# Moving the two halves of the weighted values in an attention pipeline on TensorE

## The chip, the cores and the metric

The kernel runs on one NeuronCore of a Trainium2 chip. The metric is the device time of one execution, in microseconds (us); lower is better.

## What is computed

The reference is a chain of four blocks on an input of 2 x 1024 tokens with 128 features: a two-layer transformer block with full attention, a two-layer block with local attention, a windowed attention with latent tokens, and a mixture of experts. The change is in the first block alone. Each of its layers computes, for each of the 2 sequences:

```python
xl = _ln(x, ln1_g, ln1_b)
q = (xl @ wq + bq).reshape(b_, s_, NH, DPH)          # NH = 2 heads of DPH = 64
k, v = ...                                           # likewise, from wk, bk and wv, bv
q, k = ...                                           # rotary factors, q / sqrt(DPH)
probs = jax.nn.softmax(jnp.einsum('bqhd,bkhd->bhqk', q, k), axis=-1)
att = jnp.einsum('bhqk,bkhd->bqhd', probs, v).reshape(b_, s_, h_)
x = x + att @ wo
xl2 = _ln(x, ln2_g, ln2_b)
hid = xl2 @ w1 + b1
hid = hid * jax.nn.sigmoid(1.702 * hid)
return x + hid @ w2
```

All of it is in float32.

## The kernel before

Block 1 (class `BlockA`) handles 2 layers x 2 sequences x 8 query tiles of 128 rows, 32 tiles in that order. For each tile, the following steps exist:

- `score` (L372) multiplies the tile's queries with all 1024 keys for both heads, into two PSUM tiles of 1024 columns, and VectorE takes the rows' negated maxima (L378).
- `exp(h)` (L384) is ScalarE's exponential of head h, with the row sums as a by-product.
- `turn(h, j)` (L395) transposes half j of head h's 1024 probabilities on TensorE, four 128 x 128 pieces into one PSUM bank. ScalarE copies the halves with j = 0 to SBUF (L398), VectorE those with j = 1 (L400).
- `value(j)` (L407) multiplies the transposed probabilities of key tiles 4j to 4j+3 with `v`: eight matmuls for both heads, each head in one half of the array's columns. Both halves add into one PSUM bank; `value(0)` starts the sum and `value(1)` ends it.
- `keep` (L415) copies the bank to `us` on ScalarE. With every fourth tile it starts the chain `after`.

Between these steps lies the other work on four tiles at a time, which also runs on TensorE. `after` is the rest of a layer: `project` (L442, product with `wo`; L447 and L450 on VectorE, L454 on GpSimd), a layer norm (statistics L289 and L290 on VectorE; L293 to L297 on GpSimd, where L297 writes the four normalised tiles `xn`), `turn` (L345 transposes, and ScalarE writes `hT`, L346), four times `up` (L467; L470 on ScalarE, L473 on GpSimd, L475 on VectorE), twice `down` (L488; L514 on VectorE). `prep` is the start of the next layer: the same norm, `features` (L345 and L346), `keys` (L314; L316, L317), `queries` (L321; L322) and `values` (L329; L334).

The order on each engine is the order in which the instructions are emitted, since the scheduler leaves TensorE, ScalarE, VectorE and GpSimd alone in this block. The class `Pipe` fixes it: each tile takes eight beats, and `later(beats, f, rank=...)` files a step for a later beat. In a beat the steps run by rank, the lowest first. The scores have rank 0, the chains' TensorE steps rank 5. Chain steps that need TensorE take a free beat among those that they are given, for instance `EARLY, LATE = (1, 2, 3, 5), (4, 5, 6, 7)`. So a step filed at beat 13 or 15 lies in beat 5 or 7 of the next tile's eight, and one filed at 16 lies in beat 0 of the tile after that.

PSUM has two places for scores (one for each head, used again by each tile) and four banks, called `bank`, which the transposes, the values and all steps of the chains share. A step that takes a bank waits until its former content has been read.

Of the kernel before, what the change touches and what calls it, by code (L numbers as in the profile page):

```python
# [108 lines left out]
class Pipe:  # L109
# [6 lines left out]
    def later(self, beats, f, bank=False, rank=0):  # L116
        at = self.now + beats
        if bank:
            among = range(1, 8) if bank is True else bank
            while at in self.taken or at % 8 not in among:  # L120
                at += 1
            self.taken.add(at)
        self.due.setdefault(at, []).append((rank, f))
# [54 lines left out]
class BlockA:  # L178
# [177 lines left out]
    def tile(self, l, b, qt):  # L356
        k, nc = self.k, self.k.nc
        q, kk, v = self.q[b], self.kk[b], self.v[b]
        later = self.pipe.later
        g = qt // 4  # L360
        st = self.st.setdefault((l, b, g), {})
        cut = slice(qt % 4 * P, qt % 4 * P + P)
        t = {}

        def score():
            assert ("ready", l, b, 1) in self.st or (l, b) == (0, 0)
            t["s"] = [k.ps_a.tile([P, S], F32, tag=f"s{h}", name=k.name("s")) for h in range(2)]
            for j in range(2):
                for h in range(2):
                    rows = slice(h * 64, (h + 1) * 64)  # L370
                    keys = slice(j * 512, (j + 1) * 512)
                    nc.tensor.matmul(  # L372
                        t["s"][h][:, keys], q[rows, qt * P : (qt + 1) * P], kk[rows, keys],
                        start=True, stop=True,
                    )
            t["nm"] = [self.small("nm", [1]) for _ in range(2)]
            for h in range(2):
                nc.vector.tensor_reduce(t["nm"][h], t["s"][h], AX.X, ALU.max, negate=True)  # L378

        def exp(h):  # L380
            if qt % 4 == 0 and h == 0:
                st["sums"] = self.p2.tile([P, 2, 4], F32, tag="sums", bufs=3, name=k.name("sums"))
            t["pr", h] = self.p2.tile([P, S], F32, tag="pr", bufs=4, name=k.name("pr"))
            nc.scalar.activation(  # L384
                t["pr", h], t["s"][h], AF.Exp, bias=t["nm"][h],
                accum_out=st["sums"][:, h, qt % 4 : qt % 4 + 1],
            )

        def turn(h, j):
            if h == j == 0:  # L390
                t["pT"] = self.p2.tile([P, 2, MT, P], F32, tag="pT", name=k.name("pT"))
            ps = self.bank()
            for i in range(4):
                at = (j * 4 + i) * P
                nc.tensor.transpose(ps[:, i * P : (i + 1) * P], t["pr", h][:, at : at + P], k.ident)  # L395
            dst = t["pT"][:, h, j * 4 : j * 4 + 4].rearrange("p i q -> p (i q)")
            if j == 0:
                nc.scalar.copy(dst, ps)  # L398
            else:
                nc.vector.tensor_copy(dst, ps)  # L400

        def value(j):
            if j == 0:
                t["u"] = self.bank()
            for kb in range(j * 4, j * 4 + 4):
                for h in range(2):
                    nc.tensor.matmul(  # L407
                        t["u"][h * 64 : h * 64 + 64, :P], v[:, kb, h * 64 : h * 64 + 64],
                        t["pT"][:, h, kb], start=(kb == 0), stop=(kb == MT - 1),
                    )  # L410

        def keep():
            if qt % 4 == 0:
                st["us"] = self.p2.tile([P, 512], F32, tag="us", name=k.name("us"))
            nc.scalar.copy(st["us"][:, cut], t["u"][:, :P])  # L415
            if qt % 4 == 3:
                self.after(l, b, g, st)

        for at, rank, f in (
            (0, 0, score), (3, 0, lambda: exp(0)), (4, 0, lambda: exp(1)), (9, 2, lambda: turn(0, 0)),  # L420
            (10, 2, lambda: turn(1, 0)), (11, 2, lambda: turn(0, 1)), (12, 2, lambda: turn(1, 1)),
            (13, 2, lambda: value(0)), (15, 2, lambda: value(1)), (16, -3, keep),
        ):
            later(at, f, rank=rank)

# [1820 lines left out]
```

## Time and profile before

| | |
|---|---|
| runs of the kernel, us | 1290.62, 1290.57, 1286.54 |
| median of the runs | 1290.57 us |
| the profiled execution: span from the first to the last instruction | 1288.7 us |
| mean granted TensorE clock in it | 0.962 |
| TensorE matmul busy | 1158.7 us (90%) |
| VectorE, ScalarE, GpSimd busy | 870.0, 646.3, 488.6 us (68%, 50%, 38%) |
| L407, weighted values | 73.1 us busy, 1024 matmul records |
| L395, transposes of the probabilities | 66.5 us busy, 512 records |
| L372, scores | 64.7 us busy, 256 records |

The profiled execution's own device time is not among the runs; its span of 1288.7 us is what the profile has of it, 1.9 us under the median of the runs. The profiler names the engines PE (TensorE, matmuls), PEld (its weight loads), DVE (VectorE), ACT (ScalarE), POOL (GpSimd) and SP (SyncE). A float32 matmul appears as two records, a float32 transpose as one. Matmuls are pipelined, and the ends of their records are modelled, so the time that a step costs TensorE is read from start to start. In the lines of a timeline, "x16" is a number of records that were merged, and brackets at the end name idle time of the engine and what ended it. PEclk is the clock that was granted to TensorE, 1.00 at full rate.

### The profile page before, as it was taken

The page shows a single profiled execution, that of the slowest core. Times are in us where ns is not written, and L with a number is a line of the kernel's source. Part 1 is how long each engine was busy: PE and PEld are TensorE (multiplying, and loading weights), DVE is VectorE, ACT ScalarE, POOL GpSimd, SP SyncE. Part 2 cuts the span into 40 slices and gives each one's busy share as a digit, 9 for nine tenths or more (in the row PEclk, how much of TensorE's full clock was granted, in tenths as well). Part 3 has the DMA queues.
Part 4 walks back from the last instruction along what each step waited for, and adds up shares of the span by engine and source line. Part 5 has one row for each costly group of instructions (what it writes and reads, how often), then busy time and mean ns, then how long its engine had stood idle before and what let it go on. Part 6 is the DMA issues. An engine that isn't in the chain of part 4 may idle for free.

```text
span 1288.7 us, 23486 instructions
## 1 busy us (share of the span) xinstructions
PE 1158.7 (90%) x9441; PEld 747.7 (58%) x9441; DVE 870.0 (68%) x1782; ACT 646.3 (50%) x1216; POOL 488.6 (38%) x565
## 2 busy tenths in 40 slices
PE   5999999999688999999999877989999978997798
PEld 3656766666356656666656634546555543433688
DVE  5556666555587776776777435556677979999763
ACT  5445455444355665665664545656665755441000
POOL 1523333232588776676686442221222211100000
PEclk9899999999899999999999988989998989999799
DMA  9000000000010000010100021000000000000000
GB/s 297 2 1 1 1 1 1 2 1 1 18 26 22 22 22 18 22 26 18 26 22 18 5 78 41 1 1 1 2 1 1 2 1 1 0 17 1 25 17 17
DMA packets 19840, 25.18 MB, mean 20 GB/s; under 512 B 2762, under 2 KB 13716, under 8 KB 19476
## 3 DMA queue, kind: packets, MB, share of 16 engines
q1 hardware_dynamic: 19076, 23.02, 6.4%
q8 instruction: 75, 1.23, 0.4%
q10 hardware_dynamic: 656, 0.66, 0.2%
q14 instruction: 33, 0.27, 0.1%
HBM read 13.32 MB, written 1.05 MB: 11 GB/s over the span
## 4 chain that ended last, share of the span: by engine, by line
PE 61%; DVE 23%; ACT 7%; POOL 5%; issue 4%; DMA 0%; DVEq 0%; POOLq 0%; ACTq 0%
PE big L1665 6%; PE mm L1748 5%; PE bank L407 4%; PE s L372 4%; PE bank L960 4%; PE s L727 3%; PE s L835 3%; PE bank L880 2%; PE s L1262 2%; PE s L1258 2%; PE bank L467 2%; PE tr L1299 2%; DVE nm L1267 2%; PE bank L488 2%; DVE nm L378 2%
## 5 line engine op out<-in xcount | busy, mean ns | idle before, releaser
L1267 DVE TENSOR_REDUCE nm<-s 128x4 f32<-128x1024 f32 (+1 forms) x64 | 71.0, 1152 | 60.1 <-PE s L1262 59.8
L378 DVE TENSOR_REDUCE nm<-s 128x1 f32<-128x1024 f32 x64 | 75.1, 1216 | 51.4 <-PE s L372 51.4
L1300 ACT COPY pT<-tr 128x512 f32<-128x512 f32 x120 | 70.0, 598 | 73.2 <-PE tr L1299 73.0
L774 POOL TENSOR_TENSOR t<-raw,tab 128x512 f32<-128x512 f32 x62 | 77.1, 1266 | 75.0 <-DVE raw L765 75.0
L1299 PE MATMUL tr<-ident,pr 128*128 128x128 f32 x480 | 77.2, 284 | 2.6 <-ACT pT L1300 2.3
L736 ACT ACTIVATE sq<-s 128x1024 f32<-128x1024 f32 x32 | 32.7, 1023 | 86.8 <-PE s L727 86.8
L384 ACT ACTIVATE pr<-s,nm 128x1024 f32<-128x1024 f32 x64 | 71.0, 1120 | 8.3 <-DVE nm L378 8.2
L395 PEld LDWEIGHTS bank<-ident,pr 128*128 128x128 f32 x512 | 57.4, 143 | 30.0 <-issue 22.5
L781 POOL TENSOR_TENSOR raw<-raw,tab 128x1024 f32<-128x1024 f32 x31 | 73.1, 2360 | 2.4
L788 POOL TENSOR_TENSOR raw<-raw,t 128x1024 f32<-128x1024 f32 x31 | 73.2, 2363 | 1.7
L407 PE MATMUL bank<-pT,v 128*64 128x128 f32 x1024 | 73.1, 287 | 0.7 <-DVE pT L400 0.2
L1674 ACT ACTIVATE hid<-big,cols 128x512 f32<-128x512 f32 x62 | 41.9, 687 | 60.4 <-PE big L1665 60.4
L1665 PE MATMUL big<-xTd,d_gate 128*128 128x512 f32 x128 | 67.1, 613 | 5.1 <-DVE r_above L1915 2.5
L1665 PE MATMUL big<-xTd,d_up 128*128 128x512 f32 x128 | 68.8, 628 | 2.7 <-DVE r_above L1912 2.0
L407 PEld LDWEIGHTS bank<-pT,v 128*64 128x64 f32 x1024 | 57.8, 142 | 22.6 <-issue 11.5
L398 ACT COPY pT<-bank 128x512 f32<-128x512 f32 x64 | 34.9, 587 | 68.3 <-PE bank L395 68.3
L1299 PEld LDWEIGHTS tr<-ident,pr 128*128 128x128 f32 x480 | 54.7, 144 | 21.0 <-issue 11.6
L395 PE MATMUL bank<-ident,pr 128*128 128x128 f32 x512 | 66.5, 280 | 0.0
L372 PE MATMUL s<-kk,q 64*128 64x512 f32 x256 | 64.7, 615 | 0.6 <-ACT pr L384 0.5
L1748 PEld LDWEIGHTS mm<-d_down,hid 128*128 128x128 f32 x496 | 61.0, 196 | 5.7 <-DVE xo L1779 1.9
L727 PE MATMUL s<-b_wqkv,hT 128*128 128x512 f32 x128 | 62.8, 613 | 1.7 <-ACT hT L694 1.3
L1748 PE MATMUL mm<-d_down,hid 128*128 128x128 f32 x496 | 61.7, 280 | 1.3 <-DVE xo L1779 1.3
(368 smaller groups left out, 2843.4 us busy)
## 6 DMA issues: line engine op xcount, KB each, us to landing
vs<-v SPq DMA_DIRECT2D x60, 130.0 KB, 2.2
b_wqkv<-in_L_ffn_wqkv_dram SPq DMA_DIRECT2D x2, 768.0 KB, 8.9
b_tab<-in_c_xpos_dram SPq DMA_DIRECT2D x1, 1024.0 KB, 8.0
d_up<-in_L_ffn_Wup_dram SPq DMA_DIRECT2D x1, 1024.0 KB, 5.4
d_gate<-in_L_ffn_Wgate_dram SPq DMA_DIRECT2D x1, 1024.0 KB, 7.3
out_dram<-xo SPq DMA_DIRECT2D x3, 256.0 KB, 2.3
rows<-in_rows_dram SPq DMA_DIRECT2D x1, 760.0 KB, 6.7
b_w<-in_L_ffn_w_dram SPq DMA_DIRECT2D x2, 341.0 KB, 7.7
```

Of the source, the lines that this page charges most:

```text
L372: nc.tensor.matmul(t["s"][h][:, keys], q[rows, qt * P : (qt + 1) * P], kk[rows, keys], start=True, stop=True,)
L378: nc.vector.tensor_reduce(t["nm"][h], t["s"][h], AX.X, ALU.max, negate=True)
L395: nc.tensor.transpose(ps[:, i * P : (i + 1) * P], t["pr", h][:, at : at + P], k.ident)
L407: nc.tensor.matmul(t["u"][h * 64 : h * 64 + 64, :P], v[:, kb, h * 64 : h * 64 + 64], t["pT"][:, h, kb], start=(kb == 0), stop=(kb == MT - 1),)
L727: nc.tensor.matmul(qk[:, cut], lhsT, k.b_wqkv[:, l, cut], start=True, stop=True)
L774: nc.gpsimd.tensor_tensor(t2[:, :, :, a : a + 32], r4[:, :, :, z : z + 32], tab(1)[:, :, None, a : a + 32].to_broadcast([P, 2, 8, 32]), AL ...
L781: nc.gpsimd.tensor_tensor(r4, r4, tab(0)[:, :, None, :].to_broadcast([P, 2, 8, 64]), ALU.mult)
L788: eng.tensor_tensor(flat, flat, t["t2"].rearrange("p j h d -> p (j h d)"), ALU.add)
L1267: nc.vector.tensor_reduce(nm[h], view[h], AX.X, ALU.max, negate=True)
L1299: nc.tensor.transpose(ps[:, c * P : (c + 1) * P], pr[:, c, t * P : (t + 1) * P], k.ident)
L1665: self.k.nc.tensor.matmul(ps, weights[:, rows], self.xT[:, cut], start=True, stop=True)
L1748: nc.tensor.matmul(sums[part][:, cols], hid[tp, h, c][:, e, cols], k.d_down[:, c + 8 * e, :], start=start and e == 0, stop=False,)
```

## The change

Both halves of the weighted values move to beat 16, with ranks just below that of the scores, and the copy `keep` moves from beat 16 to beat 17:

```diff
             (10, 2, lambda: turn(1, 0)), (11, 2, lambda: turn(0, 1)), (12, 2, lambda: turn(1, 1)),
-            (13, 2, lambda: value(0)), (15, 2, lambda: value(1)), (16, -3, keep),
+            (16, -1, lambda: value(0)), (16, -0.9, lambda: value(1)), (17, -3, keep),
         ):
             later(at, f, rank=rank)
```

Before, `value(0)` and `value(1)` of a tile stood in beats 5 and 7 after the next tile's scores, with the chains' steps between, behind and around them. After, both stand behind all chain steps of that stretch, in beat 0 of the tile after the next one, directly in front of its scores. No instruction is added or removed.

## The prediction

> **What bounds the kernel now.** I read the page first, then the engine's own timeline of TensorE over block 1 (22 to 322 us), then the timelines of DVE, ACT and POOL over one stretch of it, last the granted clock by one-microsecond stages. From the page:
>
> ```profile
> span 1288.7 us, 23486 instructions
> PE 5999999999688999999999877989999978997798
> L407 PE MATMUL bank<-pT,v 128*64 128x128 f32 x1024 | 73.1, 287 | 0.7 <-DVE pT L400 0.2
> ```
>
> Block 1 is the first ten slices (32.2 us each). TensorE is full there after the first slice, and the matmuls of the weighted values (L407) wait for almost nothing (0.7 us in all). So block 1 takes as long as TensorE's stream: a saving there counts in full, and so does a new hole. I call the stretch from one tile's scores (L372) to the next a round; there are 32 of them. The built order of both kernels shows rounds of four kinds that repeat: project (L442, then the turn L345 of a prep chain), queries (L314, L321, the chain's turn L345, L329, first up L467), up (three L467) and down (two L488). DVE, POOL and SP keep their order entirely, ACT too. Only TensorE's order and the PSUM banks' numbers change. Timeline of TensorE, a queries round and part of a down round (start, length to the modelled end, instruction, count; start to start is the price):
>
> ```profile
> 115.50 1.09 PE L407 MATMUL bank<-pT,v 128*64 128x128 f32 x16
> 116.52 0.68 PE L345 MATMUL bank<-ident,xn 128*128 128x128 f32 x4
> 117.04 1.06 PE L329 MATMUL bank<-a_wv,hT 128*128 128x128 f32 x8
> 118.03 1.09 PE L407 MATMUL bank<-pT,v 128*64 128x128 f32 x16
> 119.05 1.12 PE L467 MATMUL bank<-hT,a_w 128*128 128x512 f32 x2
> 120.11 1.99 PE L372 MATMUL s<-kk,q 64*128 64x512 f32 x8
> ...
> 133.14 1.95 PE L488 MATMUL bank<-a_w,hid 128*128 128x128 f32 x16
> 135.02 1.09 PE L407 MATMUL bank<-pT,v 128*64 128x128 f32 x16
> 136.05 2.05 PE L488 MATMUL bank<-a_w,hid 128*128 128x128 f32 x16
> 138.03 1.09 PE L407 MATMUL bank<-pT,v 128*64 128x128 f32 x16
> ```
>
> The reader is to see that nothing is lost between them, but that the same 16 down matmuls cost 1.88 us after a full 128x128 transpose and 1.98 us after values, which use half of the columns. A change of tile shape costs about 0.09 us: up matmuls take 0.86 us between transposes, 0.96 us with one shape change, 1.06 us with two. And a round whose values are already joined, followed by one with a hole:
>
> ```profile
> 254.31 1.97 PE L407 MATMUL bank<-pT,v 128*64 128x128 f32 x32
> 256.21 1.99 PE L372 MATMUL s<-kk,q 64*128 64x512 f32 x8
> 258.13 1.97 PE L395 MATMUL bank<-ident,pr 128*128 128x128 f32 x16
> 260.02 1.09 PE L407 MATMUL bank<-pT,v 128*64 128x128 f32 x16
> 262.54 1.76 PE L345 MATMUL bank<-ident,xn 128*128 128x128 f32 x4 [1.42 <-POOL xn L297]
> 264.23 1.98 PE L407 MATMUL bank<-pT,v 128*64 128x128 f32 x16
> 266.14 1.53 PE L467 MATMUL bank<-hT,a_w 128*128 128x512 f32 x2
> 267.60 1.99 PE L372 MATMUL s<-kk,q 64*128 64x512 f32 x8
> ```
>
> Joined values take 1.90 us, two halves 2 x 1.02 = 2.04. The hole: the turn waits for POOL's normalised tiles (L297). After it values take 1.91 us instead of 1.02 and the up 1.46 instead of 1.06. Why, the stages' clock says (us, PE busy, PEclk, DMA, GB/s):
>
> ```profile
> 262.00:263.00 1.00, 0.36 (x2) 1.00 0.00 0
> 264.00:265.00 1.00, 1.00 (x9) 0.50 0.00 0
> 267.00:268.00 1.00, 1.00 (x4) 1.00 0.00 0
> ```
>
> TensorE is mostly idle before, then its clock is halved from 263.6 to 267.0 (0.79 in the stage from 263, 0.50 in the next three), 3.4 us. The same hole stands at 76.9 and 298.4 us, three in all.
>
> **The change, part by part.** No instruction comes or goes; the values of a tile move behind everything else of their round. PSUM banks: I followed each bank's former user through the built order; all are read by then (the latest, L475's in the up rounds, are priced below). The copy L415 goes one beat later on ACT but keeps its place in ACT's order. It still waits for values that end when the scores begin, with only L398 behind it, which waits for later transposes: nothing. The chain after four tiles starts its projection at the same beat.
>
> *Up rounds (7).* Before: 9.31 us (120.11 to 129.42), with 0.4 us of waiting for L475 at 125.26. DVE reaches that after the two maxima, 5.15 us after the scores' start; this wait stays. Behind it: up 0.86, up with one change 0.96, values 1.90. 5.15 + 0.86 + 0.96 + 1.90 = 8.87: -0.44. Cover: the values' bank needs the second L475, done at 6.35 (DVE 125.72 to 126.46), values start at 6.97.
>
> *Down rounds (7).* 1.92 scores + 1.80 transposes + 1.80 + 1.89 downs + 1.90 values = 9.31 against 9.63: -0.32. Seven pairs: -0.76 x 7 = -5.3.
>
> *Two early rounds* (50.7 to 56.4 and 60.9 to 65.0 us): four and two shape changes go, and a joint: -0.40 and -0.35.
>
> *Project and queries rounds (4 pairs).* Unhindered, the project round would gain 0.11 and the queries round 0.49. But the half of the values at 115.50 stood in front of the turn at 116.52, and the turn's tiles are late: POOL's L297 runs from 115.08 to 116.82, one tile each 0.44 us. Its chain (DVE maxima, copies, L450; POOL L454 108.86 to 111.48; DVE statistics to 113.20; POOL's root) hangs on the project round's scores at 102.30 and not on TensorE's order. From that start the fourth tile is ready at 14.58 us, while TensorE now arrives at 7.55 + 1.92 + 0.49 + 0.86 + 1.31 + 0.86 = 12.99. The turn waits 1.2 us more, and behind it in TensorE's queue stand L329, the up, the values and the next scores. So the turn ends at 14.70, values' bias row L329 at 15.60, ACT's L346 (0.78 us, as at 117.24) delivers hT at 15.73, up to 16.69, values to 18.59. Before it was 17.81: +0.78 a pair, +3.1 in all. Were the tiles in time: 17.2, a gain of 0.6.
>
> *Three rounds with a hole.* Values' first half no longer stands before the turn, and the second half no longer covers ACT's L346 between turn and up. Turn at 262.54 as now, last transpose about 264.2, hT about 265.15, up 0.96, values 1.90: 268.0 at full clock. TensorE is then empty or nearly so from 260.1 to 265.15 instead of from 261.05 to 264.2. What the clock does in that, no row shows, so bounds: at full clock all the time, 268.0 against 267.60, +0.4; with one half-clock stretch as now (its loss now: 3.37 us for 2.08 of work, 1.3) 269.3, +1.7; with two, up to +3.4. The four half-clock stretches of block 1 begin at 45.1, 79.3, 263.6 and 301.1 us (from the stages), apart by 10, 54 and 11 times 3.41; so the clock is decided on a grid. The stretch from 45.1 lasted two steps: its first held 2.0 us of dense work and some scattered, and was not enough. Now a step ends anywhere from 1.8 to 5.2 us after 260.1. For 7 in 10 of these places the following step has under 2.1 us of dense work, so a second follows. Half clock then lasts 0.7 x 4.75 + 0.3 x 3.05 = 4.2 us into the work and costs half of that, 2.1: 270.1, +2.5. I take this, as the row at 45.1 is nearest: 3 x 2.5 = +7.5.
>
> The Trainium skill ("TensorE: Matmul & The Clock Gate", Part 1) states that half rate is the idle state, and that about one busy window of 3.4 us, free-running, releases it; it speaks against this change. Read with no demand on how busy, it would give one step a hole (+1.7 x 3) and a sum of +2.1; this trace's 6.8 us from 45.1 shows that a partly busy step does not release.
>
> Sum: -5.3 - 0.75 + 3.1 + 7.5 = +4.5 us. On the profiled span 1288.7 that is 1293.2; the median of the runs is 1.9 us above the span, so 1290.57 + 4.5 = 1295.1.
>
> **Rivals.** (A) One half-clock step a hole, as now: -5.3 - 0.75 + 3.1 + 5.1 = +2.1, 1292.7; without any, -1.7. For it: three holes of three did so; against: the longer emptiness. This ends within the noise, not slower. (B) The turn's tiles come earlier in the queries rounds: the place is L297 against the turn, the price 4 x 1.4 = 5.6, the point that the fourth tile be ready 1.3 us or more sooner. Then, with (A), -3.5: 1287.1; with no half clock at all, -7.3. Against: every link of L297's chain hangs on the scores, by the rows above. (C) The queries rounds drop to half clock too, from a turn stretched to 1.7 us: a 3.4 us step there is still about 70% busy, while the step from 325.0 to 328.4, with 2 us busy, kept full clock; price 1.5 each, +10.5, 1301.
>
> **How the numbers follow.** About 0.3% (3.9 us) is what this measurement can tell from no change; the three runs themselves spread over 4.1. Chances: forecast 0.47, of which 0.34 lies beyond 3.9; A 0.30 (0.06 beyond it through a longer step at one hole, 0.01 on the faster side); B 0.08 (0.05 faster by over 3.9); C 0.15. So slower 0.55, same 0.39, faster 0.06. The forecast's own range is 1292.5 (two of the holes with one step) to 1298 (two full steps, +3.4, at each hole). The range of 8 in 10 is 1290.0 to 1299.5: below it reaches to A with one hole that keeps full clock (1292.7 - 1.3) and 1.4 for a queries round's wait that is 0.35 us shorter in each pair; above to the forecast's upper end and one queries round of C. Outside stay B and the most of C.
>
> **What would show it.** Up and down rounds of 8.87 and 9.31 us; project plus queries 18.6 with the turn waiting for L297 for over a microsecond; the three holes with a turn idle of 2.4 us, an up waiting for L346, and half clock for over 3.4 us. Wrong, if the queries rounds' turn does not wait, if half clock lasts 3.4 us as before, or if block 1's end (proj at 322.05) moves by something else than +4.5 while the rest of the span moves too.

## The result and the profile after

Over 22 runs each, the changed kernel takes 1290.33 us (median; 1288.01 to 1296.48), the kernel before 1288.28 us (1281.48 to 1290.66). The ratio is 1.0023, with a 95% interval of 1.0012 to 1.0034: slower by about 3 us, where 4.5 us were forecast; the medians differ by 2.05 us. The forecast of 1295.1 us stood on a median of three runs, 1290.57 us, and lies 4.8 us above the measured one.

From the page of the profiled execution after (its time was 1294.39 us, at the upper end of the runs):

```profile
span 1292.6 us, 23486 instructions
PE 5889999988778999999999877989999978997798
L407 PE MATMUL bank<-pT,v 128*64 128x128 f32 x1024 | 66.5, 283 | 0.5 <-DVE pT L400 0.2
```

The values are busy for 66.5 us instead of 73.1, but TensorE's row now dips to 8 in slices 1, 2, 8 and 9, counted from 0. The timeline of TensorE after, a queries round from its turn on, and the end of a down round:

```profile
115.51 1.62 PE L345 MATMUL bank<-ident,xn 128*128 128x128 f32 x4
116.97 1.06 PE L329 MATMUL bank<-a_wv,hT 128*128 128x128 f32 x8
118.00 1.13 PE L467 MATMUL bank<-hT,a_w 128*128 128x512 f32 x2
119.06 1.97 PE L407 MATMUL bank<-pT,v 128*64 128x128 f32 x32
120.95 1.99 PE L372 MATMUL s<-kk,q 64*128 64x512 f32 x8
...
133.64 3.74 PE L488 MATMUL bank<-a_w,hid 128*128 128x128 f32 x32
137.31 1.97 PE L407 MATMUL bank<-pT,v 128*64 128x128 f32 x32
```

The four transposes of the turn stretch over 1.46 us, where they took 0.52: the turn has caught up with GpSimd's tiles, which come as early as before (115.08 us there, from project scores at 102.30; here from scores at 102.24):

```profile
115.01 1.74 POOL L297 TENSOR_SCALAR xn<-xi,mn,rs 128x128 f32<-128x128 f32 x4
```

The two downs take 3.67 us together instead of 1.88 + 1.98, the values 1.90 instead of 2 x 1.02. A hole after, in the same view:

```profile
257.01 1.99 PE L372 MATMUL s<-kk,q 64*128 64x512 f32 x8
258.93 1.97 PE L395 MATMUL bank<-ident,pr 128*128 128x128 f32 x16
263.34 1.76 PE L345 MATMUL bank<-ident,xn 128*128 128x128 f32 x4 [2.44 <-POOL xn L297]
265.97 2.07 PE L467 MATMUL bank<-hT,a_w 128*128 128x512 f32 x2 [0.87 <-ACT hT L346]
267.97 3.29 PE L407 MATMUL bank<-pT,v 128*64 128x128 f32 x32
271.19 1.99 PE L372 MATMUL s<-kk,q 64*128 64x512 f32 x8
```

And the stages' clock there (us, PE busy, PEclk, DMA share, GB/s):

```profile
263.00:264.00 1.00, 0.56 (x2) 0.94 0.00 0
265.00:266.00 1.00, 0.13 (x2) 0.50 0.00 0
269.00:270.00 1.00, 1.00 (x14) 0.50 0.00 0
271.00:272.00 1.00, 1.00 (x10) 1.00 0.00 0
```

The turn waits 2.44 us instead of 1.42, the up waits 0.87 us for ScalarE where it waited for nothing, and the clock stays halved for 6.83 us instead of 3.41. Of the three holes after, this one has two such steps; the other two have one, as before.

Where the time goes, round by round (scores to scores, us; both profiled executions):

| | before | after | forecast after |
|---|---|---|---|
| up round | 9.32 | 8.97 | 8.87 |
| down round | 9.63 | 9.28 | 9.31 |
| project and queries rounds together | 17.81 | 18.71 | 18.59 |
| second early round | 8.68 | 8.32 | 8.33 |
| the three holes' rounds | 11.33, 11.39, 11.54 | 13.41, 14.18, 13.23 | 2.5 more each |
| first scores to last projection | 299.89 | 305.26 | +4.5 |
| last projection to the end | 966.65 | 966.68 | as before |

### The profile page after: what moved, and what is told of

The parts are those of the page before. It is cut to its first block, busy times and chain, and to the rows that moved or that the text cites. A ratio compares the mean times of both kernels' runs of the same rounds, so it can differ in the third digit from the quotient of the medians.

```text
span 1292.6 us, 23486 instructions
## 1 busy us (share of the span) xinstructions
PE 1153.7 (89%) x9441; PEld 747.9 (58%) x9441; DVE 869.1 (67%) x1782; ACT 645.8 (50%) x1216; POOL 488.4 (38%) x565
## 3 DMA queue, kind: packets, MB, share of 16 engines
HBM read 13.32 MB, written 1.05 MB: 11 GB/s over the span
## 4 chain that ended last, share of the span: by engine, by line
PE 59%; DVE 23%; ACT 7%; POOL 6%; issue 4%; DMA 0%; DVEq 0%; POOLq 0%; ACTq 0%
PE big L1665 6%; PE mm L1748 5%; PE bank L407 4%; PE bank L960 4%; PE s L372 3%; PE s L727 3%; PE s L835 3%; PE bank L880 2%; PE s L1262 2%; PE s L1258 2%; PE bank L467 2%; PE tr L1299 2%; DVE nm L1267 2%; DVE nm L378 2%; PE bank L488 2%
## 5 line engine op out<-in xcount | busy, mean ns | idle before, releaser
L781 POOL TENSOR_TENSOR raw<-raw,tab 128x1024 f32<-128x1024 f32 x31 | 73.1, 2359 | 2.4
L407 PE MATMUL bank<-pT,v 128*64 128x128 f32 x1024 | 66.5, 283 | 0.5 <-DVE pT L400 0.2
```

Of the source, the lines that this page charges most:

```text
L407: nc.tensor.matmul(t["u"][h * 64 : h * 64 + 64, :P], v[:, kb, h * 64 : h * 64 + 64], t["pT"][:, h, kb], start=(kb == 0), stop=(kb == MT - 1),)
L781: nc.gpsimd.tensor_tensor(r4, r4, tab(0)[:, :, None, :].to_broadcast([P, 2, 8, 64]), ALU.mult)
```

## The experiments

Times are medians, ratios are to the kernel before in runs on the same chip. Most kernels change only the places of `value(0)`, `value(1)` and `keep`; the three places of the old order are (13, 2), (15, 2), (16, -3), those of the new one (16, -1), (16, -0.9), (17, -3).

**The new order for half of the tiles.** One kernel uses the new places for two of each four tiles, another for the other two:

```diff
+        front = qt % 4 >= 2          # e2: qt % 4 < 2
+        places = ((16, -1), (16, -0.9), (17, -3)) if front else ((13, 2), (15, 2), (16, -3))
```

> The new order for the tiles with qt % 4 of 2 or 3 alone (up rounds, down rounds and the two early rounds); the other tiles keep the old order. My account of the rounds (gains in up and down rounds, losses in queries rounds and at the holes): up rounds 8.97 us and down rounds 9.3 us as in the changed kernel, project plus queries 17.8 and the holes as before, so 7 x 0.65 + 0.4 = about 5 us less than before, mean about -5. Rival (the change's time is the half-clock grid's position and the rounds themselves sum to nothing): within 1.5 us of before.

> The new order for the tiles with qt % 4 of 0 or 1 alone (project and queries rounds, rounds with a hole). Account of the rounds: queries pairs 18.7 instead of 17.8 (+3.6) and holes +5 to +7.5, up and down rounds 9.3 and 9.6 as before: +8 to +11 us over before. Rival (holes cost little on average): +4 to +5.

Measured: up, down and early rounds alone 1279.96 us, 0.9936 (0.9916 to 0.9955); project, queries and hole rounds alone 1298.90 us, 1.0085 (1.0061 to 1.0109). In their profiles the moved rounds are as long as in the changed kernel (8.97, 9.28; 7.57 + 11.15), the others as before. The change is two opposite changes in one. The gain, 8 us, is larger than the 5 us expected from the rounds; that is taken up below.

**Idle TensorE filled at the holes.** In front of the late turn, between its tiles and in front of the first up stand transposes of the identity, into PSUM that is overwritten afterwards:

```diff
         for i in range(4):
+            for _ in range(fill[min(i, 1)]):      # 21 and 2 (after), 12 and 2 (before)
+                nc.tensor.transpose(ps[:, i * P : (i + 1) * P], k.ident, k.ident)
...
+            for _ in range(6 if alone and c == 0 else 0):      # changed order alone
+                nc.tensor.transpose(ps[:, :P], k.ident, k.ident)
             nc.tensor.matmul(ps, k.a_w1[:, l, c * P : (c + 1) * P], hT, start=True, stop=True)
```

> The changed kernel with idle TensorE time at the three holes filled by transposes of the identity whose results are overwritten (21 in front of the turn, 2 before each further tile, 6 in front of the up). If half clock is what the longer holes add, there is no half-clock stretch at the holes, the span from the hole's scores to the next is 11.7 to 11.9 us instead of 13.2 to 14.2, and the kernel is 4 to 6 us faster than the changed one (1.4 to 2.4 at each hole). If it is only the wait itself, it gains nothing.

> The kernel before with the holes filled in the same way (12 transposes of the identity in front of the turn, 2 before each further tile). Half clock at the holes goes: hole rounds 10.1 us instead of 11.4, 3 to 4 us less than before on average. The difference of filled changed kernel and this one is then the deterministic part of the change: 3 x 1.75 + 3.6 - 4.7 = +4.2. Rival: the fill itself delays the turn and gains nothing.

Measured: filled changed kernel 1282.72 us, 0.9959 (0.9944 to 0.9975); filled kernel before 1279.99 us, 0.9937 (0.9920 to 0.9954). Neither profile has a half-clock stretch before the last projection. Timeline of TensorE, the same hole in the filled changed kernel:

```profile
257.65 2.46 PE L346 MATMUL bank<-ident 128*128 128x128 f32 x21
...
261.70 0.82 PE L474 MATMUL bank<-ident 128*128 128x128 f32 x6
262.74 1.12 PE L475 MATMUL bank<-hT,a_w 128*128 128x512 f32 x2 [0.21 <-ACT hT L348]
263.79 1.97 PE L409 MATMUL bank<-pT,v 128*64 128x128 f32 x32
265.69 1.99 PE L374 MATMUL s<-kk,q 64*128 64x512 f32 x8
```

(Its line numbers are a few higher.) (In this cut the four tiles of the turn, from 260.25 to 261.70 us, are left out.) The turn's first tile comes no sooner after the scores than without the fill, 6.32 and 6.33 us, and the up 0.15 us sooner, but the up now takes 1.05 us instead of 2.00 and the values 1.90 instead of 3.22. The holes' rounds last 11.76 to 11.79 us here and 9.95 to 9.97 in the filled kernel before: without any half clock the change costs 1.8 us a hole. Half clock costs 1.4 to 1.6 us a hole in the old order (11.33 to 11.54 less 9.96) and 1.4 to 2.4 in the new one. The first early round, free of half clock in both, is 14.76 in the old and 14.22 in the new order, a gain of 0.54; in the table's two executions a half-clock stretch lay over it and hid that (15.90 and 16.32). From first scores to last projection the filled pair differs by 297.72 - 294.37 = 3.35 us, in time by 2.7. Both gained more than was expected (8 us against the kernel before where 3 to 4 were, 7.6 against the changed one where 4 to 6 were): in their profiles the stretch behind block 1 is also 5 us shorter than in the two executions of the table above.

**One kind of round put back at a time.**

```diff
+        front = not (l, b, qt) in ((0, 0, 5), (1, 1, 1), (1, 1, 5))                    # holes back
+        front = qt % 4 != 1 or (l, b, qt) in ((0, 0, 5), (1, 1, 1), (1, 1, 5))         # queries back
```

> The changed kernel, but the three tiles whose values stand in a round with a hole (tiles 5, 25 and 29 of the 32) keep the old order. Account of the rounds: 3.67 (queries pairs) - 4.9 (up and down) - 0.9 (early rounds) = -2.1 us against before, with hole rounds of 11.3 to 11.6 us as before; so the holes would carry +5.5 of the change and more where half clock is longer. Rival (the queries rounds carry the loss): within 1 us of the changed kernel.

> The changed kernel, but the tiles whose values stand in the four queries rounds (9, 13, 17 and 21) keep the old order. Account of the rounds: the pair falls from 18.7 to 17.7 us, 4 x 1.0 less than the changed kernel, so about -0.6 against before, with the spread that the half-clock grid gives. Rival (the turn is late there whatever stands ahead of it): the pair stays at 18.7 us.

Measured: holes back 1280.28 us, 0.9948 (0.9930 to 0.9965), holes' rounds 10.97, 11.22 and 9.97, the last without half clock. Queries back 1290.80 us, 1.0013 (0.9998 to 1.0029). There the turn is nearly in time again, 0.61 us from its start to that of L329, by TensorE's timeline:

```profile
115.34 1.09 PE L407 MATMUL bank<-pT,v 128*64 128x128 f32 x16
116.36 0.77 PE L345 MATMUL bank<-ident,xn 128*128 128x128 f32 x4
116.97 1.06 PE L329 MATMUL bank<-a_wv,hT 128*128 128x128 f32 x8
```

and the pair of rounds is 7.57 + 10.22 = 17.79 us. That is 3.7 us less in four pairs, but the whole kernel's time did not show it. Both expectations for the whole kernel missed: -2.1 and -0.6 us against before were expected, the medians moved by -8.4 and +2.2. In the two profiles block 1 itself, from first scores to last projection, takes 295.46 and 301.81 us, both less than the 305.26 of the changed kernel: a first sign that the time is not the sum of block 1's rounds.

**Both halves together, but in front of the first up.**

```diff
-            (16, -1, lambda: value(0)), (16, -0.9, lambda: value(1)), (17, -3, keep),
+            (15, 2, lambda: value(0)), (15, 2.1, lambda: value(1)), (16, -3, keep),
```

> Both halves stand together in beat 7 with rank 2, in front of a first up, instead of directly in front of the scores. Only the wait of the first up for ACT's L346 is covered again, not the turn's wait for POOL's L297. Account: hole rounds 0.7 us shorter each than in the changed kernel at equal clock (the wait of 0.87 goes, two shape changes come back), queries pairs still 18.7, up and down rounds 8.97 and 9.28: 2 us less than the changed kernel, +1 against before. Rival (the second half of the values matters nothing): as the changed kernel.

Measured: 1289.11 us, 1.0012 (0.9998 to 1.0025). Holes' rounds 12.47, 12.04 and 12.21 us with one half-clock step each; the up has no wait. The changed order's holes with one step as well take 13.2 to 13.4 us in all profiles, so about 1.1 us of the longer round belongs to the uncovered wait for L346 (0.7 was expected); the turn's wait (still 2.44 us) is the rest against the old order. That the wait for L346 also makes a second step likelier fits these three holes, but three do not show it. In time, 1 us more than before was expected and 1.5 measured.

**Gains together.** The new order in up, down and early rounds, with the holes filled as in the filled kernel before (the edits of both):

> The new order for the tiles with qt % 4 of 2 or 3 alone, and the holes filled with transposes of the identity as in the filled kernel before. The two gains lie in different rounds and should add: 5.2 to 5.7 us less than the filled kernel before (span 1272, about 1274.5 in time), so some 14 us less than before, with a spread of 3 us instead of 7. Rival (the gains share the same half-clock time): about 1279.

Measured: 1278.01 us (1272.31 to 1279.88), 0.9919 (0.9896 to 0.9942), the fastest kernel of the study, but 3.5 us above the 1274.5 expected and nearer to the rival's 1279. In block 1 the gains do add (288.59 us from first scores to last projection, 294.37 in the filled kernel before, 5.8 less), but from there to the end it took 966.41 us, where five of the other profiles show 960.5 to 961.8.

**The place on the clock's grid.** That difference leads to the missing part of the size. All half-clock stretches of a profile begin on a grid of 3.41 us. Ordered by where the grid stands when block 1 ends (start of the next half-clock stretch less start of the last projection, modulo 3.41), the time from that projection to the end is, over the thirteen profiles of whole kernels, with the part of it that ran at half clock:

| place, us | time to the end, us | of it at half clock, us | kernels |
|---|---|---|---|
| 0.08 | 960.50 | 64.9 | holes back |
| 0.30 | 964.22 | 78.5 | new order for qt % 4 < 2 |
| 0.79 to 1.24 | 961.23, 961.41, 961.63, 961.76 | 71.7, 71.7, 68.3, 68.3 | changed and 1.9 us late; filled after; filled before; new order for qt % 4 >= 2 |
| 1.87, 2.10 | 962.38, 962.59 | 68.3, 71.7 | before and 1.0 us late; before and 1.9 us late |
| 2.52 to 2.97 | 966.24, 966.41, 966.68, 966.59, 966.65 | 81.9 in each | before the up; the fastest; changed; queries back; before |

Busy times of the stretch behind block 1, as windows (start and end, length, busy time and count of PE, PEld, DVE, ACT and POOL, PEclk, DMA share, GB/s), of the kernel before, the changed one, and the one with the holes back:

```profile
322.05:1288.70 966.65, 860.37 (x7103) 547.61 (x7101) 679.12 (x1403) 488.05 (x920) 382.53 (x382) 0.96 0.06 16
```

```profile
325.92:1292.60 966.68, 860.20 (x7103) 547.70 (x7101) 679.00 (x1403) 488.13 (x920) 381.72 (x381) 0.96 0.06 16
```

```profile
317.20:1277.70 960.50, 853.91 (x7103) 543.32 (x7101) 679.25 (x1403) 488.08 (x920) 381.95 (x381) 0.97 0.06 16
```

The same instructions, within 1 us the same time on DVE, ACT and POOL, but TensorE busy for 6.5 us less in the third. So blocks 2 to 4 cost up to 6 us more or less with the half clock that falls into them, and in these profiles, but for the one at 0.30, that goes with the place at which block 1 hands over. Whether that place can be shifted on purpose, three kernels with extra transposes in front of the last projection asked:

```diff
             pj = [self.bank(), self.bank()]
+            for _ in range(17 if last else 0):      # e10: 9
+                nc.tensor.transpose(pj[0][:, :P], k.ident, k.ident)
```

> The kernel before with 17 transposes of the identity (17 x 0.1125 = 1.9 us, their result overwritten) in front of block 1's last projection; nothing else. Theory: blocks 2 to 4 take 960.5 to 966.7 us, set by where on the half-clock grid block 1 ends (ten profiles: a grid edge 2.5 to 3.0 us after the projection's start, taken modulo 3.41: 966.2 to 966.7; 0.1 to 1.25 us: 960.5 to 961.8, once 964.2), and the half-clock stretches at the holes carry block 1 to nearly the same place in most runs. The shift then takes 2.9 to 1.0: the runs that stood at 1288 to 1290.6 fall by about 3 (1.9 more in block 1, 5 less behind it), the median to 1285 or 1286. Rival (the place is random from run to run, the spread is noise): median +1.9, 1290.5.

> The same with 9 transposes, 1.0 us. Theory: the edge falls at about 1.9 us, a place that no profile has shown; between 1.25 (961.8) and 2.5 (966.2), so anything from -4 to +1.0 us against before, and the profile's own place and rest tell which. Rival: +1.0 us.

> The changed kernel with the same 17 transposes, 1.9 us. Theory: its runs near 1294 (edge at 2.8 us, rest 966.7) fall by about 3, those near 1288 (rest about 961) rise by 2 to 7; which way the median goes tells how its runs are spread over the grid. Rival: +1.9 us, 1292.

Measured: 1287.59 us, 1.0007 (0.9992 to 1.0023); 1286.74 us, 1.0013 (0.9994 to 1.0031); 1293.29 us, 1.0049 (1.0031 to 1.0068). The profiles fit the table, the place of 1.9 us foreseen for the second among them, but the theory that most runs hand over at one place falls: the first median does not drop by 3 us, the intervals of the first two hold the rivals' +1.9 and +1.0 as well as nothing, and the third rises by about 3 over the changed kernel. How much half clock falls into a run varies: over the twelve runs of the second kernel the granted clock lies from 0.962 to 0.969 and the time from 1293.4 to 1284.9 us.

**Block 1 by itself.** Four kernels end after block 1 (the lines of blocks 3 and 4 go as well; they stand at the dots):

```diff
             stage_a(k, masks, b)
-        stage_b(k, b)
...
+            b.out["rest"]()
+            tc.nc.sync.dma_start(out.rearrange("(i p) d -> p i d", p=P), k.xo)
```

> Block 1 alone in the old order; blocks 2 to 4 are left out and block 1's result is written to the output. About 322 + 5 us. It is the base for the other three. By the holes seen so far (9.96 at full clock, 10.95 to 11.6 with a half-clock step) runs should lie within 4 us of each other, and not in two groups 4 us apart as the whole kernel's.

> Block 1 alone in the new order; blocks 2 to 4 are left out. If block 1 loses what the rounds sum to, +5 to +6.5 us against block 1 alone in the old order, and the later blocks gave some back. Rival (the profiles stand at unlike places): +2 to +3.

> Block 1 alone with the new order in up, down and early rounds; blocks 2 to 4 are left out. By the rounds -5.3 us against the old order. Rival (block 1 itself gains the 8 us that the whole kernel showed): -8.

> Block 1 alone in the new order but for the four queries rounds; blocks 2 to 4 are left out. By the rounds 3.3 us less than the new order throughout. Rival (the queries rounds' wait costs nothing, as the whole kernel's time seemed to say): no difference.

| block 1 alone (4 or 5 runs each) | median, us | range | against the old order | whole kernel, same edit |
|---|---|---|---|---|
| old order | 350.99 | 350.61 to 352.53 | | |
| new order | 357.15 | 356.45 to 358.72 | +6.2 | +2.05 (medians) |
| new order in up, down, early rounds | 346.36 | 344.52 to 348.15 | -4.6 | -8.7 |
| new order but for queries rounds | 352.58 | 351.75 to 355.57 | +1.6 | +2.2 |

(The length of 351 instead of 327 holds the first steps of block 2, which block 1 files, and the output.) Block 1 alone moves by what its rounds sum to, within about 1 us, and runs lie within 2 to 4 us instead of 8. So the change costs block 1 about 6 us, and about 4 us of that (by the medians; 2.7 by the means, 1287.5 us over 95 runs and 1290.8 over 22 for the whole, 351.3 and 357.3 for block 1) come back behind it. The granted clock, which each run lists, says in what form. In the profiles it is 1.00 or 0.50 and nothing else, so 2 x (1 - mean clock) x span is a run's time at half clock. Block 1 alone spends 21.1 us in it in the old order and 29.2 in the new (means); the whole kernel 89.9 us before (73 runs) and 89.4 changed (22 runs). Block 1 gains about 8 us of half clock and the whole kernel none, so blocks 2 to 4 hold about 8 us less.

## Why the prediction was right or wrong

*What bounds block 1: right.* TensorE's stream was the time: block 1 alone moved by what its rounds sum to, within about 1 us.

*Up and down rounds: right in kind, 0.1 us too large in one.* 9.32 to 8.97 and 9.63 to 9.28, together -0.70 a pair instead of -0.76, -4.9 us in seven pairs instead of -5.3. In the up round the last two ups after the wait take 1.91 us, not 0.86 + 0.96. The cause, fewer changes of tile shape, fits the downs, but no experiment separated it from the joint itself.

*Early rounds: right.* -0.54 (free of half clock, in the filled pair) and -0.36, against -0.40 and -0.35.

*Project and queries rounds: right.* The turn caught up with L297 and ended 14.73 us after the project round's scores (14.70 forecast), and the pair rose by 0.90 instead of 0.78: +3.6 instead of +3.1. Putting those tiles back returned the pair to 17.79.

*Holes: right.* Waits of 2.44 and 0.87 us, as told. At full clock the forecast has the round at 268.0 - 256.21 = 11.79 us, and filled it took 11.76 to 11.79. Over six profiles with the new order at the holes, 10 of 18 half-clock stretches lasted two steps (7 in 10 were forecast); with the old order, seven profiles, none of 20, and one hole had no half clock. The three rounds grew by 6.5 us in the two profiled executions, and in block 1 alone from 11.41, 11.40, 11.55 to 13.34, 14.06, 14.44: +7.5, the forecast's figure. Rival A, one step always, is ruled out; so are B (the turn did wait) and C (no half clock in any queries round).

*The sum of block 1: somewhat low.* 4.5 forecast, 5.4 in the two profiles, 6.2 in block 1 alone.

*The step that failed: the last one, "the median of the runs is 1.9 us above the span, so 1290.57 + 4.5 = 1295.1".* It carries block 1's sum over to the whole kernel as it stands, and takes two things for granted. First, that three runs' median is the kernel's time. Over 22 runs it was 1288.28, since the runs lie from 1281.5 to 1290.7. The profiled execution, with a span of 1288.7 us at clock 0.962, is one of the longest: of the 73 runs before whose clock is on record, 11 had that clock, and they took 1290.1 to 1290.6 us. Second, that blocks 2 to 4 cost the same after any block 1: the sum has no term for them, and no reason is given. In the two profiles they did (966.65 and 966.68, at places 2.97 and 2.83), over the runs they did not: block 1 loses 6.2 us alone and the kernel 2 to 3.3, with about 8 us less half clock behind block 1. The prediction had the grid in hand, but priced it at the three holes only and not in the blocks behind.

*Luck.* The measured 1290.33 lies inside the range of 8 in 10, at its lower edge, but that edge stood for one half-clock step or none at each hole and shorter waits in the queries rounds, and neither came. The lower end of the forecast's own range, 1292.5 for two holes with one step, does not follow from its terms either: -5.3 - 0.75 + 3.1 + 2 x 1.7 + 2.5 is +2.95, so 1293.5.

*What stays open.* That the time behind block 1 goes with the half clock in it is shown by thirteen profiles. That the place on the grid sets it is only a fit, with one profile (0.30 us) off the order, and the shifts of 1.0 and 1.9 us did not move the medians by it. Why the blocks behind the changed block 1 hold less half clock on average is not shown: the place of a run is known only where it was profiled.

## What to carry to other kernels

Work that stands in front of a late operand is a cover: before it is moved back, look up when the operand is ready, and put in the moved length. Where a reorder gains in some rounds and loses in others, it can be made for those alone: here the same three numbers give 1280 us instead of 1290 when half of the tiles use them. And a difference of a few us between kernels that fall in and out of half clock needs either many runs or the stretch timed by itself (block 1 alone lost 6.2 us where the whole kernel showed 2 to 3.3); one profile of each says what happens in a round, not what the median will be.

## What the runs showed of the hardware

- A hole costs time after it too: in the old order TensorE waits 1.42 us in it, and the half clock that follows costs 1.4 to 1.6 us more; in the new one, with waits of 2.44 and 0.87 us, the half clock costs 1.4 to 2.4. Filling the idle time with useless transposes, without starting anything sooner, made the kernel before 8 us faster (0.9937, 0.9920 to 0.9954); 4.4 us of that lie in the holes' rounds of the profiles.
- Half-clock stretches come in whole steps: 3.41, 6.83, 10.24 and once 17.07 us in each of the thirteen profiles of whole kernels (one is broken off by the program's end). The kernel before spreads over 9 us (1281.5 to 1290.7), and its granted clock goes with it: 0.962 at 1290.1 to 1290.6 us, 0.964 at 1287.8 to 1289.5, 0.969 at 1283.2 to 1283.6. Filled, six runs lay within 2.7 us. The Trainium skill ("TensorE: Matmul & The Clock Gate", Part 1) states the free-running window of about 3.4 us, and these steps agree.
- At the very start the matmuls run at half rate although PEclk shows 1.00: in the kernel before, four 512-column key records from 15.74 us took 3.57 us, 0.89 each, and two from 112.37 us took 0.86, 0.43 each. The time at which this ends differs from one execution to the next: the profiles' first record of the clock stands at 17.9 to 21.3 us, and the first scores began at 20.4 to 22.2 us.
- Each change between a tile of the full array and a divided one went with about 0.09 us (downs 1.88 and 1.98 us; the pair 3.67 together, with two changes less). No run separates the change of shape from the joint between two groups of matmuls.
